# Message passing over 400,000 edges on one core: the last 23 supertiles' messages kept in DRAM, three slot tables in turn, 0/1 rows made by ScalarE

## The chip, the core and the metric

The kernel runs on one core of a Trainium2 chip. The metric is the device time of one execution in microseconds (us); three runs of the kernel before lie within 7 us of each other. The core's engines work side by side, each through its own instructions in order: PE (TensorE, matrix products, with PEld its weight loads), DVE (VectorE), ACT (ScalarE), POOL (GpSimd) and SP (SyncE, which here only issues transfers). Transfers run on 16 DMA engines and are issued by SP, by ACT and, where rows go to computed addresses, by POOL.

## What is computed

Nodes are 12,500 rows of 128 numbers, edges 400,000, sorted by `dst`:

```python
h   = relu(layernorm(x)) @ W_in2f.T
Wij = (smu(f_ij @ W_f1.T + b_f1) @ W_f2.T + b_f2) * rcut_ij[:, None]
agg = segment_sum(h[dst] * Wij, src, 12500)      # gathered by dst, summed by src
out = x + smu(agg @ W_o1.T + b_o1) @ W_o2.T + b_o2
# smu(z) = ((1+a) z + (1-a) z erf(mu (1-a) z)) / 2, a = 0.01, mu = 2.5
```

The edges are sorted by the index of the gather, so that one needs only a narrow window of `h`; the sum goes by the random index `src`.

## The kernel before

**Tiles.** 128 edges are a tile (3125 of them), four tiles a group (`GRP`, 782 groups), eight tiles a supertile (`SUP`, 391). Supertiles are cut into nine epochs by `PARTS` (59 supertiles each at first, 16 in the last). 128 nodes are a bin (98 bins).

**One edge group.** `load` (L432) brings the edge attributes, the row of relative targets (`rbc`) and a window of `h` by the SP queue. `pick` (L465) compares the row with the partition number (`prow`; `pcol` for the first six supertiles) into a 0/1 matrix `oh`, once for a supertile, on DVE (L472). `gather` (L585) multiplies the window by it on PE, `take` (L600) copies the result to SBUF on ACT. `hide`, `bend`, `smooth`, `weigh` (L556 to L617) make the filter: PE, ACT (Gelu), DVE, PE. `mix` (L621) multiplies both on DVE. `turn` (L630) multiplies each tile by `w_o1` on PE, which also brings edges onto partitions. `send` (L639) scales by the edge weight on ACT into an `ms` buffer (six of them, L642), puts the node's number inside its bin beside it as a 129th column, and has POOL scatter the 128 rows of each tile to their slots by an indirect DMA (L649).

**Slots.** Each epoch has its own DRAM table `buf` (L103) with `CAP[k]` rows for each bin. `bins`, `count`, `read`, `number` (L482 to L552) compute each edge's slot: running counts on DVE, a triangular product on PE, a maximum on DVE. `so` holds the running counts and chains from group to group. The rows that may stay empty are cleared before the epoch by SP from a tile of zeros (`clear`, L168).

**Adding up.** During epoch k the table of epoch k-1 is read back by SP (`fetch`, L673, four chunks ahead), DVE makes a 0/1 selection `se` by comparing the 129th column with `irow_ps` (`choose`, L684) and PE multiplies rows and selection into a bin's sum (`add`, L695: one product for each 128 slots, `Q[k]` of them for a bin), which DVE adds to `agg`. `parts` (L725) spreads these products over the groups of the epoch.

**Order.** The order on PE, DVE, ACT and SP is the program's (L282). The main loop (L901) runs once for each group g: `turn(g)` and `send(g)`, then `number`, `weigh`, `gather`, `take`, some `parts`, `mix` for g+1, `hide`, `bend`, `count`, `smooth` for g+2, `pick` for a supertile ahead, `bins(g+3)`, `read(g+2)`, more `parts`. In epoch 0 a list of `steps` (layernorm and `h` of all nodes, the index rows) is interleaved.

**The end.** After the loop the last epoch's table is added up (L960 to L1044), and each unit of four bins goes through Gelu on ACT, an addition on POOL (L1000), `w_o2` on PE, an addition on DVE and its store. The old rows `x` of 12 units are read ahead during the last epoch (`ahead`, L928), the others by ACT's queue at the end; POOL adds the output bias to them (L250).

Of the kernel before, what the change touches and what calls it, by code (L numbers as in the profile page):

```python
# [9 lines left out]
F32 = mybir.dt.float32  # L10
# [9 lines left out]
P = 128  # L20
# [11 lines left out]
PARTS = (59, 59, 59, 59, 48, 37, 27, 27, 16)  # L32
# [8 lines left out]
def gnn_kernel(  # L41
# [46 lines left out]
    for a, n in eps_of:  # L88
        mean = n * SUP * P * P / N
        dev = SIGMA * math.sqrt(mean)  # L90
        CAP.append(math.ceil((mean + dev) / P) * P)
        ZMIN.append(max(0, math.floor((mean - dev) / ZP) * ZP))
# [10 lines left out]
    bufs = [dram.tile([NB * CAP[k], ROW], F32, name=f"buf{k}") for k in range(EPOCHS)]  # L103
# [17 lines left out]
    nc.vector.tensor_add(prow, prow, late)  # L121
    irow = const.tile([P, P], F32, name="irow")
# [19 lines left out]
    b1w = const.tile([P, P], F32, name="b1w")  # L142
# [14 lines left out]
    b2row = const.tile([1, P], F32, name="b2row")  # L157
    b1 = const.tile([P, 1], F32, name="b1")
    bz = const.tile([P, 1], F32, name="bz")
    w_o1 = const.tile([P, P], F32, name="w_o1")  # L160
# [4 lines left out]
    zero = const.tile([ZP, CB * max(c - z for c, z in zip(CAP, ZMIN)) * ROW // ZP], F32, name="zero")  # L165
# [109 lines left out]
    with tc.tile_pool(name="ld", bufs=4) as ld, \  # L275
# [8 lines left out]
        irow_ps = ps1.tile([P, GRP * P], F32, name="irow_ps")[:, 0:P]  # L284
# [138 lines left out]
        def last_loads():  # L423
            nc.sync.dma_start(b2row, b_f2)
            nc.sync.dma_start(bo2, b_o2.to_broadcast([P, P]))

        groups = [(t0 + a, g) for t0, nt in sups for a, g in chunks(nt, GRP)]
        epoch = [k for k, (a, n) in enumerate(eps_of) for _ in range(n)]
# [3 lines left out]
        def load(s):  # L432
            if s >= NS:
                return
            t0, nt = sups[s]
            e0, n = t0 * P, nt * P
            fb = fbufs[s % NF]
# [28 lines left out]
        def pick(s):  # L466

            if s >= NS:
                return
            n = sups[s][1] * P  # L470
            oh = edge.tile([P, SUP * P], BF, name="oh", bufs=3)
            nc.vector.tensor_scalar(oh[:, :n], loaded[s][1][:, :n], pcol if s < FEW // SUP else prow, None, op0=ALU.is_equal)  # L472
            onehot[s] = oh

        last = {}
        begins = {}

# [4 lines left out]
        def bins(g):  # L482


            if g >= NG:
                return
            t, n = groups[g]
            so = cnt.tile([P, GRP, NB], F16, name="so")
            if g in first:
                k = first[g]  # L490
                m = FEW if g == 0 else tiles_of(k)
                begins[k] = (t, cnt.tile([P, max(n for _, n in eps_of) * SUP], F32, name="hic", bufs=2))
                nc.vector.tensor_scalar(begins[k][1][:, :m], hi_f[:, t:t + m], float(CAP[k]), -BIG, op0=ALU.mult, op1=ALU.add)
                last[0] = none
            before = last[0]
# [3 lines left out]
            last[0] = so[:, n - 1]  # L499
            bins_of[g] = (before, so)  # L500
# [43 lines left out]
        def number(g):  # L544
            if g >= NG:
                return
            (t, n), k = groups[g], epoch[g // PER]
            t0, hic = begins[k]
            ix = cnt.tile([P, GRP], I32, name="ix", bufs=8)
# [80 lines left out]
        def turn(g):  # L630

            n = groups[g][1]
            pt = ps1.tile([P, GRP, P], F32, name="pt")
            mt = mixed.pop(g)
            for j in range(n):
                nc.tensor.matmul(pt[:, j, :], mt[:, j * P:(j + 1) * P], w_o1, start=True, stop=True)  # L636
            mixed[g] = pt

        def send(g):  # L639
# [3 lines left out]
            nc.scalar.activation(ms[:, :n, P], lo_b[:, t:t + n], AF.Copy)  # L643
            pt = mixed.pop(g)
            for j in range(n):
                nc.scalar.activation(ms[:, j, 0:P], pt[:, j], AF.Copy, scale=w_sb[:, t + j:t + j + 1])  # L646
            k, ix = epoch[g // PER], taken.pop(g)
# [36 lines left out]
        def choose(k, c):  # L684
# [6 lines left out]
            nc.vector.tensor_tensor(se[:, :m], irow_ps.unsqueeze(1).to_broadcast([P, m, P]),  # L691
# [3 lines left out]
        def add(k, b, q):  # L695
# [15 lines left out]
            if g == GRP - 1 or b == NB - 1:  # L711
                dst = agg[:, (b - g) * P:(b + 1) * P]
                src = pgs[0][:, :g + 1].rearrange("p b n -> p (b n)")
                if k == 0:
                    nc.vector.tensor_copy(dst, src)
                else:
                    nc.vector.tensor_add(dst, dst, src)  # L717

# [15 lines left out]
        def homes():  # L734
            spent = eps_of[-1][0] * SUP // (GRP * P) * (GRP * P)
            for t in (w_sb, hi_f):
                for o in range(0, spent, GRP * P):
                    yield t[:, o:o + GRP * P]
            for o in range(0, spent // 2 // (GRP * P) * (GRP * P), GRP * P):
                yield lo_w.bitcast(F32)[:, o:o + GRP * P]  # L740

        held = {unit: home.rearrange("p (b d) -> p b d", b=GRP)
                for unit, home in zip([u for u in units if u[1] == GRP][::2], homes())}
        ahead = list(held)
# [85 lines left out]
        def output_bias():  # L830

            nc.vector.tensor_scalar(w_o2, w_o2, GC, None, op0=ALU.mult)
            nc.vector.tensor_scalar(bz, b1, ZS, None, op0=ALU.mult)
            nc.vector.tensor_scalar(b1w, onesb, b1, LIN, op0=ALU.mult, op1=ALU.mult)
            pb1 = bank("pb1")[:, 0, :]
            nc.tensor.matmul(pb1, b1w, w_o2, start=True, stop=True)
# [64 lines left out]
        for g in range(NG):  # L901
            s = g // PER
            k = epoch[s]
            g0, ng = eps_of[k][0] * PER, min(eps_of[k][1] * PER, NG - eps_of[k][0] * PER)
            i = g - g0
            if g == (FEW // SUP - 3) * PER:
                assert not opening
            if g % PER == 0:
                load(s + 3)
# [7 lines left out]
            elif k + 1 < EPOCHS:  # L917
# [5 lines left out]
            if k and i == 0:  # L923
                work = [(b, q) for b in range(NB) for q in range(Q[k - 1])]
                done = 0
# [4 lines left out]
            if k and k == EPOCHS - 1 and i >= WAIT and ahead:  # L930
                unit = ahead.pop(0)
                old_rows(unit, held[unit], nc.sync)
            lo = hi = 0
# [4 lines left out]
            if g:  # L938
# [3 lines left out]
            number(g + 1)  # L942
            weigh(g + 1)
            gather(g + 1)
            take(g + 1)
            parts(k - 1, lo + (hi - lo) // 2)
            mix(g + 1)
            step()
            hide(g + 2)
            bend(g + 2)  # L950
            count(g + 2)
            smooth(g + 2)
            if g % PER == 0:
# [5 lines left out]
            assert k == 0 or taken_steps == COUNT  # L959
        k = EPOCHS - 1  # L960
# [5 lines left out]
        small = [u for u in units if u[0] >= NB // GRP * GRP]  # L966
        row_of, ready, opened, smoothed, summed = [], [], [], [], []
        wanted = small + [u for u in units if u not in small]

        def ask():  # L970
            if wanted:
                unit = wanted.pop(0)
                name = ("hg", "mt")[len(wanted) % 2]
                if unit in held:
                    xr = held[unit]
                else:
                    xr = edge.tile([P, GRP * P], F32, name=name).rearrange("p (b d) -> p b d", b=GRP)
                    old_rows(unit, xr, nc.scalar)
                with_bias(unit, xr, nc.gpsimd)
                row_of.append((unit, xr))  # L980
# [28 lines left out]
        def store():  # L1009
            unit, py = summed.pop(0)  # L1010
            was, xr = row_of.pop(0)
            assert was == unit
            stored(unit, py, xr, msg.tile([P, GRP, ROW], F32, name="ms")[:, :, 0:P], nc.sync)
            ask()

        while ahead:
            unit = ahead.pop(0)
            old_rows(unit, held[unit], nc.sync)
        for _ in range(4):
            ask()  # L1020
# [40 lines left out]
    with tc.If(flag > 0):  # L1061
        with tc.tile_pool(name="gl", bufs=1) as gl, tc.tile_pool(name="gps", bufs=1, space=PSUM) as gps:
# [3 lines left out]
            for b, n in chunks(N + P, P):  # L1066
                nc.sync.dma_start(tab[b:b + n, :], zt[:n])
            drop = gl.tile([P, 1], F32, name="drop")
# [125 lines left out]
```

## Time and profile before

| | |
|---|---|
| median of 3 runs | 4111.01 us (4106.05 to 4113.0) |
| the profiled execution | 4114.52 us |
| its span, first to last instruction | 4112.7 us |
| granted TensorE clock, mean | 0.976 |
| HBM read, written | 442.34 MB, 373.37 MB |

The span is what the views of the profile divide up; the 1.8 us between it and the execution's time lie outside the first and last instruction. A row of a view by lines names source line, engine, operation, tiles out and in, shapes and count, then busy time in us and the mean ns of one, then the idle time ahead of it with what ended it. A row of a view by windows has busy time and number of instructions for each engine in that stretch, the clock, the DMA engines' mean share and the GB/s moved. In a timeline the first two columns are start and duration in us.

### The profile page before, as it was taken

The numbers are of one execution on the slowest core, as the hardware profiler recorded it, in microseconds if no ns is written. First come the engines' busy times: TensorE is split into PE (matmuls) and PEld (weight loads), VectorE is DVE, ScalarE is ACT, GpSimd is POOL, SyncE is SP. The second block draws the span as 40 slices with busy tenths as digits, with TensorE's granted clock in tenths as the row PEclk, the third lists the DMA queues.
The fourth block names the chain that finished last, engine by engine and source line by source line (L and its number), as shares of the span: only waits on it lengthen the run. The fifth ranks groups of instructions, "written<-read, shape, count | busy, mean of one in ns | idle before, by whom it ended". The sixth has DMA issues, their size and how long they took to land.

```text
span 4112.7 us, 74065 instructions
## 1 busy us (share of the span) xinstructions
PE 3675.1 (89%) x21113; PEld 2552.3 (62%) x21117; DVE 3450.5 (84%) x7657; ACT 1944.9 (47%) x5690; POOL 3096.4 (75%) x3199
## 2 busy tenths in 40 slices
PE   7878887999888998979999979999899989999898
PEld 4445545666655666646666656666677767666678
DVE  8988776888878888868888868888799979888897
ACT  4457754444444444435444434444444434444442
POOL 6777777777777777777777777777777777777775
PEclk9999998999999999989999989999999999999999
DMA  6866656766647666646766647777688789887668
GB/s 187 231 187 182 191 166 183 213 202 195 188 141 219 198 201 197 199 146 196 212 199 187 199 148 207 210 204 211 176 228 223 195 230 242 221 228 221 176 195 248
DMA packets 564245, 820.83 MB, mean 200 GB/s; under 512 B 178033, under 2 KB 378488, under 8 KB 563698
## 3 DMA queue, kind: packets, MB, share of 16 engines
q1 hardware_dynamic: 456096, 604.98, 53.5%
q0 software_dynamic: 100320, 207.40, 15.7%
q10 hardware_dynamic: 7410, 3.65, 0.3%
q8 instruction: 167, 2.74, 0.3%
q14 instruction: 252, 2.06, 0.2%
HBM read 442.34 MB, written 373.37 MB: 198 GB/s over the span
## 4 chain that ended last, share of the span: by engine, by line
PE 39%; DVE 29%; DMA 18%; ACT 6%; issue 5%; POOL 2%; DVEq 0%; ACTq 0%; POOLq 0%; SPq 0%
DMA buf<-ms,ix 17%; PE pt L636 11%; PE pg L704 9%; PE pw L616 8%; DVE se L691 8%; PE pu L563 7%; DVE mt L626 5%; DVE so L497 5%; DVE sm L579 3%; DVE sl L541 3%; ACT ge L571 2%; ACT ms L646 2%; PE ph L597 2%; POOL buf L649 2%; DVE agg L717 1%
## 5 line engine op out<-in xcount | busy, mean ns | idle before, releaser
L649 POOL DMA_INDIRECT buf<-ms,ix x3125 | 3025.4, 968 | 972.7 <-issue 395.9
L646 ACT ACTIVATE ms<-pt,w_sb 128x128 f32<-128x128 f32 x3125 | 888.8, 368 | 1125.5 <-PE pt L636 1118.0
L636 PE MATMUL pt<-w_o,mt 128*128 128x128 f32 x6250 | 881.3, 284 | 390.9 <-DVE mt L626 388.4
L704 PEld LDWEIGHTS pg<-se,rw 128*128 128x128 f32 x8036 | 1052.4, 192 | 249.7 <-issue 210.8
L704 PE MATMUL pg<-se,rw 128*128 128x128 f32 x8036 | 1148.8, 280 | 4.5 <-DVE se L691 3.7
L636 PEld LDWEIGHTS pt<-w_o,mt 128*128 128x128 f32 x6250 | 765.5, 193 | 478.7 <-DVE mt L626 474.5
L497 DVE SCALAR_TENSOR_TENSOR so<-irow_ps,hi_f,so 128x98 f16<-128x98 f32 x3116 | 989.0, 317 | 82.7
L616 PE MATMUL pw<-sm,w_f 128*128 128x512 f32 x1564 | 826.7, 611 | 10.4 <-DVE sm L579 8.5
L563 PE MATMUL pu<-f,w_f 128*128 128x512 f32 x1564 | 811.4, 601 | 0.0
L626 DVE SCALAR_TENSOR_TENSOR mt<-pw,b,hg 128x512 f32<-128x512 f32 x782 | 583.6, 746 | 207.3 <-ACT hg L605 203.8
L571 ACT ACTIVATE ge<-pu 128x512 f32<-128x512 f32 x782 | 468.6, 599 | 532.7 <-PE pu L563 526.5
L579 DVE SCALAR_TENSOR_TENSOR sm<-pu,ge 128x512 f32<-128x512 f32 x782 | 535.3, 684 | 187.8 <-ACT ge L571 182.0
L691 DVE TENSOR_TENSOR se<-irow_ps,rw 128x1536 f32<-128x1536 f32 (+1 forms) x345 | 587.9, 1704 | 114.3 <-DMA rw<-buf 110.2
L605 ACT ACTIVATE hg<-ph 128x512 f32<-128x512 f32 x782 | 468.6, 599 | 62.1 <-PE ph L597 44.9
L541 DVE TENSOR_REDUCE sl<-pc 128x4 f32<-128x392 f32 x782 | 434.7, 556 | 0.0
L643 ACT ACTIVATE ms<-lo_b 128x4 f32<-128x4 bf16 x782 | 159.9, 204 | 358.7 <-DMA buf<-ms,ix 358.2
L597 PE MATMUL ph<-oh,hw 126*128 126x512 bf16 x770 | 298.3, 387 | 0.0
L563 PEld LDWEIGHTS pu<-f,w_f 128*128 128x128 f32 x1564 | 253.5, 196 | 53.4 <-issue 43.8
L511 PE MATMUL pc<-so,tri 128*128 128x392 f16 x782 | 257.9, 330 | 1.0 <-DVE sl L541 0.8
L616 PEld LDWEIGHTS pw<-sm,w_f 128*128 128x128 f32 x1564 | 241.1, 195 | 24.7 <-DVE sm L579 21.4
L513 PEld LDWEIGHTS <-rest_h 128*128 128x128 f16 x781 | 76.5, 98 | 265.9 <-issue 265.9
L513 PE MATMUL pc<-so,rest_h 128*128 128x294 f16 x781 | 225.1, 288 | 0.0
(161 smaller groups left out, 1391.0 us busy)
## 6 DMA issues: line engine op xcount, KB each, us to landing
rw<-buf SPq DMA_DIRECT2D x292, 774.0 KB
rbc<-rel_dram SPq DMA_DIRECT2D x389, 256.0 KB
buf<-zero SPq DMA_DIRECT2D x243, 387.0 KB
buf<-ms,ix POOLq DMA_INDIRECT x3125
buf<-zero SPq DMA_DIRECT2D x193, 258.0 KB
rw<-buf SPq DMA_DIRECT2D x49, 645.0 KB
f<-in_f_t SPq DMA_DIRECT2D x390, 80.0 KB
hw<-h_dram SPq DMA_DIRECT2D x770, 31.5 KB
```

The costliest lines, as they stand in the source:

```text
L497: nc.vector.scalar_tensor_tensor(so[:, j], irow_ps[:, :NB], hi_f[:, t + j:t + j + 1], so[:, j - 1] if j else before, op0=ALU.is_equal, op1 ...
L541: nc.vector.tensor_reduce(sl[:, :n], pc[:, :n], op=ALU.max, axis=AX.X)
L563: nc.tensor.matmul(pu[:, :n], w_f1, loaded[g // PER][0][:, o:o + n], start=True, stop=True)
L571: nc.scalar.activation(ge[:, :n], units_of[g][:, :n], AF.Gelu, scale=ZS)
L579: nc.vector.scalar_tensor_tensor(sm[:, :n], units_of.pop(g)[:, :n], LIN, hidden[g][:, :n], op0=ALU.mult, op1=ALU.add)
L616: nc.tensor.matmul(pw[:, :n], w_f2, hidden.pop(g)[:, :n], start=True, stop=True)
L626: nc.vector.scalar_tensor_tensor(mt[:, :n], pws.pop(g)[:, :n], b2, rows_of.pop(g)[:, :n], op0=ALU.add, op1=ALU.mult)
L636: nc.tensor.matmul(pt[:, j, :], mt[:, j * P:(j + 1) * P], w_o1, start=True, stop=True)
L646: nc.scalar.activation(ms[:, j, 0:P], pt[:, j], AF.Copy, scale=w_sb[:, t + j:t + j + 1])
L649: i = nc.gpsimd.indirect_dma_start(out=bufs[k][:, :], out_offset=bass.IndirectOffsetOnAxis(ap=ix[:, j:j + 1], axis=0), in_=ms[:, j, :], in ...
L691: nc.vector.tensor_tensor(se[:, :m], irow_ps.unsqueeze(1).to_broadcast([P, m, P]), rows_in[c][:, :m, P:P + 1].to_broadcast([P, m, P]), op= ...
L704: nc.tensor.matmul(pgs[0][:, g, :], rows_in[c][:, o, 0:P], sel[c][:, o, :], start=(q == 0), stop=(q == Q[k] - 1))
```

## The change

There are ten epochs; the last two (`SENT_LAST`), 16 and 7 supertiles, 181 tiles, are "kept". Their groups are computed in the main loop, one supertile after every ninth of supertiles 59 to 265 (`flow`), and their message rows are written by ACT's DMA queue to `kept_rows` in DRAM; their slot numbers stay in `ix_kept`. After the main loop the rows are read back by SP (`refill`), POOL scatters them, and during that the tables of epochs 7 and 8 are added up. The tables are three stores used in turn; a mark added to the 129th column (`mark`, `marks`) tells the rows of an epoch from older ones, so only the first three epochs clear. The 0/1 rows `oh` are made by ACT as relu(1 - |row - prow|), two passes for a group, from the seventh supertile on. Messages that aren't kept are only transposed by PE (`turn`), and `w_o1` is applied to `agg` at the end of epoch 7 (`fold`). All old rows and the bias for them come ahead of the end, the bias on DVE.

```diff
-PARTS = (59, 59, 59, 59, 48, 37, 27, 27, 16)
+PARTS = (59, 59, 59, 59, 48, 37, 27, 20, 16, 7)
+SENT_LAST = 2
+BUFS = 3
...
-    bufs = [dram.tile([NB * CAP[k], ROW], F32, name=f"buf{k}") for k in range(EPOCHS)]
+    stores = [dram.tile([NB * CAP[k], ROW], F32, name=f"buf{k}") for k in range(min(BUFS, EPOCHS))]
+    bufs = [stores[k % BUFS][0:NB * CAP[k], :] for k in range(EPOCHS)]
...
+        flow, rest_of = [], list(range(EARLY, NS))
+        start, gap = eps_of[1][0], (eps_of[5][0] - eps_of[1][0]) // (NS - EARLY)
+        for s in range(EARLY):
+            flow.append(s)
+            if s >= start and (s - start) % gap == gap - 1 and rest_of:
+                flow.append(rest_of.pop(0))
+        flow += rest_of
...
-            rb = ld.tile([P, SUP * P], BF, name="rbc")
+            rb = ld.tile([P, SUP * P], BF, name="rbc", bufs=3)
...
+        def pick_part(g):
...
+            s, i = divmod(g, PER)
+            if s < FEW // SUP:
+                if i == 0:
+                    pick(s)
+                return
+            if i == 0:
+                onehot[s] = edge.tile([P, SUP * P], BF, name="oh", bufs=3)
+            o, n = i * GRP * P, groups[g][1] * P
+            oh = onehot[s][:, o:o + n]
+            nc.scalar.activation(oh, loaded[s][1][:, o:o + n], AF.Abs, bias=nrow)
+            nc.scalar.activation(oh, oh, AF.Relu, scale=-1.0, bias=onesb[:, 0:1])
...
             for j in range(n):
-                nc.tensor.matmul(pt[:, j, :], mt[:, j * P:(j + 1) * P], w_o1, start=True, stop=True)
+                if s_of(g) < EARLY:
+                    nc.tensor.transpose(pt[:, j, :], mt[:, j * P:(j + 1) * P], ident)
+                else:
+                    nc.tensor.matmul(pt[:, j, :], mt[:, j * P:(j + 1) * P], w_o1, start=True, stop=True)
...
+            if s_of(g) >= EARLY:
+                nc.scalar.dma_start(kept_rows[:, t - kept_tile:t - kept_tile + n, :], ms[:, :n, :])
+                return
+            scatter(g, ms)
...
+        def fold():
+
+            dst = plain.pop(0)
+            w = dst.shape[1]
+            po = ps1.tile([P, GRP * P], F32, name=("pu", "ph")[len(folded) % 2])
+            nc.tensor.matmul(po[:, :w], w_o1, dst, start=True, stop=True)
+            nc.scalar.activation(dst, po[:, :w], AF.Copy)
+            folded.append(w)
...
-            elif k + 1 < EPOCHS:
+            elif k + 1 < BUFS:
...
+            if s < EARLY:
+                k = chores(g)
+            else:
+                lo = hi = done
...
-            if g % PER == 0:
-                pick((g + 4) // PER)
-            bins(g + 3)
-            read(g + 2)
+            pick_part(at(p + 4))
+            bins(at(p + 3))
+            read(at(p + 2))
...
+        def refill(g):
+            if g < NG:
+                t, n = groups[g]
+                back[g] = msg.tile([P, GRP, ROW], F32, name="ms")
+                nc.sync.dma_start(back[g][:, :n, :], kept_rows[:, t - kept_tile:t - kept_tile + n, :])
+
+        g1 = EARLY * PER
+        for g in range(g1, g1 + 4):
+            refill(g)
+        for g in range(g1, NG):
+            refill(g + 4)
+            k = chores(g)
+            scatter(g, back.pop(g))
+            parts(k - 1, hi)
+            if g - g1 >= 2:
+                old(g - g1 - 2)
+            biased(g - g1 - 10)
```

`chores(g)` holds what stood at the head of the loop's body: clearing, the beginning of an epoch and the share of `parts` due in group g. `scatter` is the second half of what `send` did.

More of the change, by code (lines that the diff above doesn't have):

```diff
@@ L91, in gnn_kernel @@
         CAP.append(math.ceil((mean + dev) / P) * P)
-        ZMIN.append(max(0, math.floor((mean - dev) / ZP) * ZP))
+        ZMIN.append(max(0, math.floor((mean - dev) / ZP) * ZP) if len(ZMIN) < BUFS else 0)
+    assert all(c <= CAP[k % BUFS] for k, c in enumerate(CAP)) and (EPOCHS - 1) // BUFS < GRP
     Q = [c // P for c in CAP]
@@ L121, in gnn_kernel @@
     nc.vector.tensor_add(prow, prow, late)
+    nrow = const.tile([P, 1], F32, name="nrow")
+    nc.vector.tensor_scalar(nrow, prow, -1.0, None, op0=ALU.mult)
     irow = const.tile([P, P], F32, name="irow")
@@ L487, in bins @@
             t, n = groups[g]
-            so = cnt.tile([P, GRP, NB], F16, name="so")
+            kept = s_of(g) >= EARLY
+            so = cnt.tile([P, GRP, NB], F16, name="so_kept" if kept else "so", bufs=2 if kept else 3)
             if g in first:
@@ L937, in gnn_kernel @@
                 hi = upto * (i + 1 - WAIT) // (ng - WAIT)
-            if g:
+            return k
+        k = 0
+        for p in range(len(seq)):
+            g = seq[p]
+            s = g // PER
+            if p == (FEW // SUP - 3) * PER:
+                assert not opening
+            if p % PER == 0:
+                load(sup_at(p // PER + 3))
+            if s < EARLY:
+                k = chores(g)
+            else:
+                lo = hi = done
+            if p:
                 turn(g)
@@ L963, in gnn_kernel @@
         choose(k, order_of[k][0])
[L966 to L980, printed above, removed]
+        ready, opened, smoothed, summed = [], [], [], []
         turns = [0, 0]
@@ L1010, in store @@
             unit, py = summed.pop(0)
-            was, xr = row_of.pop(0)
+            was, xr = rows_got.pop(0)
             assert was == unit
             stored(unit, py, xr, msg.tile([P, GRP, ROW], F32, name="ms")[:, :, 0:P], nc.sync)
[L1014 to L1020, printed above, removed]
         for c in order_of[k]:
```

139 lines of the change are left out of this document (91 added, 48 removed).

## Prediction

> **What bounds the kernel now.** I read the page first, then the scatter alone, then single iterations. The page's shares mislead:
>
> ```profile
> PE 3675.1 (89%) x21113; PEld 2552.3 (62%) x21117; DVE 3450.5 (84%) x7657; ACT 1944.9 (47%) x5690; POOL 3096.4 (75%) x3199
> L649 POOL DMA_INDIRECT buf<-ms,ix x3125 | 3025.4, 968 | 972.7 <-issue 395.9
> ```
>
> PE looks the fullest and POOL idles 972.7 us. The timeline of POOL alone, and the scatter's own view with windows, say otherwise:
>
> ```profile
> 1999.34 0.96 POOL L649 DMA_INDIRECT buf<-ms,ix  x1 [0.30 <-issue]
> 2000.61 0.96 POOL L649 DMA_INDIRECT buf<-ms,ix  x1 [0.30 <-ACT ms L643]
> 2001.87 0.96 POOL L649 DMA_INDIRECT buf<-ms,ix  x1 [0.31 <-DMA buf<-ms,ix]
> L649 POOL DMA_INDIRECT buf<-ms,ix x3125: 956/962/1460, 19.9 to 4022.2; - x196
> 20.00:560.00 540.00, 404.92 (x414) 0.97 0.70 198
> 560.00:3400.00 2840.00, 2159.04 (x2235) 0.98 0.68 195
> 3400.00:3870.00 470.00, 355.60 (x368) 0.99 0.80 218
> 3870.00:4024.00 154.00, 105.78 (x110) 1.00 0.71 201
> ```
>
> A scatter starts every 1.265 us: 0.96 busy and 0.30 of idle time that recurs whatever is named as its releaser, so it belongs to the instruction. 3124 such periods are 3952 us; the first scatter starts at 19.9, the last at 4022.2, so only 50 us in 4002 are anything else. Stage by stage (length less count x 1.265): 16 us to 560, 13 to 3400, 4.5 to 3870, 14 in the last epoch (to 4023). The engines' loads differ between epochs, the scatter does not:
>
> ```profile
> 2000.00:2500.00 500.00, 441.62 (x2525) 306.57 (x2525) 404.84 (x890) 226.63 (x676) 380.32 (x394) 0.97 0.63 187
> 3000.00:3500.00 500.00, 477.41 (x2915) 347.36 (x2914) 441.77 (x932) 230.00 (x679) 378.06 (x393) 0.98 0.85 223
> ACT ms L643 <- DMA buf<-ms,ix: 358.2, 163, 6.2
> ```
>
> PE goes from 441.62 to 477.41 us in 500, POOL does 394 and 393 scatters. The third row, of the waits, is the back pressure: ACT waits 358 us for one of the six `ms` buffers to be scattered. So POOL is the bound until 4022, and then a tail of 90 us follows, without scatters. Whatever the change saves on PE and DVE in the main loop is worth nothing by itself; it counts where POOL stands still, where a scatter is stretched, and in the tail.
>
> **The change, part by part.**
>
> *POOL's work*: 3125 scatters as before, 2944 in the main loop, 181 behind it; 0 us. The clears that go (some 89 MB, by SP) lay beside POOL: 0.
>
> *The comparison leaves DVE.* What stretches a scatter shows in single places:
>
> ```profile
> 1302.27 1.22 POOL L649 DMA_INDIRECT buf<-ms,ix  x1 [0.30 <-issue]
> 1302.18 0.48 DVE L472 TENSOR_SCALAR oh<-rbc,prow 128x1024 bf16<-128x1024 bf16 x1
> ```
>
> The scatter that begins 0.09 us into a comparison takes 1.22 us, not 0.96. All stretching together is at most 3025.4 - 3125 x 0.962 = 19 us; by the windows some 6.5 of it lies before 560, where other DVE work stretches too. From 560 on it is 2159.04 + 355.60 - 2603 x 0.962 = 11 us. I take a gain of 13 (8 to 19).
>
> The Trainium skill, page "SBUF — State Buffer", section "Who interferes with whom", says that a VectorE instruction in a 2-port mode and GpSimd exclude each other, the later one blocking fully. Held for a whole comparison (0.48 us) on each of 385, that would be a gain of some 185 us; the measured stretch of 19 us in all decides against that size, while the trace agrees with the sign.
>
> *ACT gets two passes for each group.* No row shows this operation. The nearest:
>
> ```profile
> L353 ACT ACTIVATE hs<-pg 128x512 bf16<-128x512 f32 x6 | 3.6, 595 | 0.0
> L994 ACT ACTIVATE ge<-agg,bz 128x512 f32<-128x512 f32 x24 | 17.0, 721 | 52.2 <-DVE ms L268 22.1 <-POOL hg L250 16.8 <-DVE agg L717 7.2
> L226 ACT ACTIVATE hs<-rw 128x512 bf16<-128x512 f32 x23 | 14.9, 647 | 1.8 <-DVE rw L223 1.8
> ```
>
> So 1.19 to 1.44 us for two; I take 1.3, by L226 (source and target in SBUF). They stand behind `bend` on ACT, and the next `send` is queued behind them.
>
> *PE transposes.* The turn's row has two instructions for a tile, a transpose one:
>
> ```profile
> 2005.47 1.06 PE L636 MATMUL pt<-w_o,mt 128*128 128x128 f32 x8
> 304.66 0.60 PE L211 MATMUL pg<-ident,rw 128*128 128x128 f32 x4
> 2006.36 1.02 PE L616 MATMUL pw<-sm,w_f 128*128 128x512 f32 x2
> 2012.12 0.59 PE L616 MATMUL pw<-sm,w_f 128*128 128x512 f32 x1
> ```
>
> Eight passes are issued in 0.89 us (2005.47 to 2006.36), 0.111 each; four transposes, 0.60 in all, need half. PE saves 0.45 us for each early group: hidden behind POOL.
>
> *Is the loop fast enough for POOL?* Eighteen early groups give POOL 18 x 4 x 1.265 = 91.1 us of work, but beside them two kept groups are computed: twenty iterations in 91.1 us, 4.55 each. Per iteration (98.5 in the window 2000 to 2500):
>
> ```profile
> L704 PE MATMUL pg<-se,rw 128*128 128x128 f32 x978 | 145.3, 281 | 0.0
> L472 DVE TENSOR_SCALAR oh<-rbc,prow 128x1024 bf16<-128x1024 bf16 x48 | 23.9, 498 | 0.0
> L691 DVE TENSOR_TENSOR se<-irow_ps,rw 128x1536 f32<-128x1536 f32 x41 | 71.8, 1752 | 19.1 <-DMA rw<-buf 18.9 <-PE pg L704 0.2
> L717 DVE TENSOR_TENSOR agg<-agg,pg 128x512 f32<-128x512 f32 (+1 forms) x21 | 14.0, 667 | 0.7 <-PE pg L704 0.7
> ```
>
> PE 441.62/98.5 = 4.48, less 0.45: 4.03; DVE 4.11 less 23.9/98.5: 3.87; ACT 2.30 + 1.3 = 3.60. Kept iterations have no `parts` but the old turn: PE 4.48 less 978 x 0.111/98.5 = 1.1, that is 3.4, DVE 4.11 - 0.24 - 0.87 = 3.0. Over twenty, PE asks 3.97 (87% of 4.55), DVE 3.78 (83%), ACT 3.60 (79%). Before, at POOL's 5.08, the shares were 88%, 81% and 45%, with 0.46 us of back pressure for each iteration (358/782). So POOL just stays fed; I take 0, and up to +90 if the chain through the fuller ACT lengthens iterations (first rival).
>
> *Epoch 0.* There ACT also makes `h`:
>
> ```profile
> 300.00:560.00 260.00, 221.54 (x1130) 137.84 (x1129) 209.07 (x506) 192.41 (x538) 198.17 (x204) 0.99 0.64 188
> ```
>
> 51 groups x 1.3 us on 192.4 busy make 259 of 260 us: ACT becomes the bound. At nine tenths of its time (PE reaches 0.88 and 0.95 in the windows above) the stretch takes some 288 us, 28 more; up to 30 us of it (24 scatters waiting in six `ms` buffers) is absorbed. Between 0 and +30 I take +10.
>
> *The last epochs.* The 14 us lost after 3870 came from 258 `add` products in 28 groups, 9.2 each, when PE could not keep up. The densest stage of the main loop now is 294 in 36, 8.2, with 0.45 us less of other PE work; I take 5 of 14, and beside it the 4.5 us before 3870 as now: gain 9 (0 to 14).
>
> *The refill.* Behind the loop 181 x 1.265 = 229 us of scatters go on, each fed from DRAM. SP's queue holds the refills and the table reads in one order, and a table read waits for PE; POOL has four groups (20 us) ahead. By the size of a chunk (below, 1536 rows) epochs 7 and 8 read 19.4 and 12.9 MB, refills 12.0, old rows 6.4, scatters 12.0: 62.7 MB in 229 us, 274 GB/s.
>
> ```profile
> 4031.00:4108.00 77.00, 68.60 (x585) 67.10 (x584) 59.03 (x68) 17.68 (x26) 44.61 (x37) 0.98 0.90 273
> rw<-buf SPq DMA_DIRECT2D x292, 774.0 KB
> ```
>
> The tail of before moved 273 GB/s at 0.90 of the DMA engines' time: full would be 303. At 223 GB/s and 0.85 (the window from 3000), full is 262, and the stage takes 239. So 0 to +35; I take +5.
>
> *The tail.* It runs from the last scatter to the end:
>
> ```profile
> 4022.18 0.96 POOL L649 DMA_INDIRECT buf<-ms,ix  x1 [0.30 <-issue]
> 4031.55 1.76 DVE L691 TENSOR_TENSOR se<-irow_ps,rw 128x1536 f32<-128x1536 f32 x1 [1.46 <-DMA rw<-buf]
> ```
>
> 9.4 us until the last table's rows are there, then 81 to the span's end for 25 units, of which I put 75, 3.0 each, to the units and 6 to draining. A unit was 16 passes of `add` and 8 of `w_o2` on PE, 24 x 0.111 = 2.7 us, and 0.53 MB of table, 0.26 out and 0.26 of old rows. With one product for a bin it is 16 passes, 1.8 us; on DVE 0.69 + 0.69 + a third of a `se` 0.58 = 1.96; 0.53 MB at 303 GB/s 1.75. I take 2.0: 9.4 + 50 + 6 = 65, a gain of 25 (15 to 32).
>
> **Sum** against the profiled execution, 4114.5: -13 + 10 - 9 + 5 - 25 = -32, and of the 16 us lost before 560 and the 4.5 later nothing else moves: 4082. The median of the runs shown is 3.5 lower than that execution: 4079.
>
> **The rivals.**
>
> 1. *ACT takes POOL's place between supertiles 68 and 265* (slower). A comparison of 1.3 us now stands between `bend` and the next `send`; where DVE's `se` (1.75 us) makes `mix` late, ACT has little left to catch up: the gap ahead of `send` is about as long as the two passes.
>
> ```profile
> 2006.56 0.63 ACT L646 ACTIVATE ms<-pt,w_sb 128x128 f32<-128x128 f32 x2 [1.27 <-PE pt L636]
> ```
>
> Price: 23 stretches x (18 e + 2 x 3.8 - 91.1) for an early iteration of e. It starts to cost at 4.64 us and makes the kernel slower than before at 4.73 (40/23/18 more). At 4.85 it is 23 x 3.8 = 87: 4166. For it: the iteration with a `se` from 2006.36 to 2012.12, above, took 5.76 us. Against it: PE's 0.45 and DVE's 0.24 us less.
>
> 2. *The refill stage is bound by transfers.* At the profile's mean of 200 GB/s, 62.7 MB take 313 us, not 229: 4158. For it: rows get shorter, three and two slots a partition. Against it: 273 GB/s in the tail now.
>
> 3. *The tail and the stretching don't follow*: the tail stays bound by latencies, and other DVE work stretches scatters as much. Without 25 of the 38 gained: 4104.
>
> 4. *Abs, Relu and Gelu in turn reload ACT's tables.*
>
> ```profile
> L413 ACT ACT_TABLE_LOAD x1 | 1.3, 1283 | 2.6 <-issue 2.6
> ```
>
> Two for each group would be 776 x 2 x 1.28 = 1990 us on ACT, over its slack by far: about 5500. Only four loads stand in this trace, though Copy and Gelu alternate; that is the case against. The Trainium skill, "ScalarE: Activation LUTs", section "Table sets: the hidden batching unit", has relu, abs, copy and identity in every set, and by that rule no load is added; no run so far shows Abs.
>
> **How the numbers follow.** Forecast 0.62 (4050 to 4103), rival 1 0.18, rival 2 0.08, rival 3 0.11, rival 4 0.01. The low end takes the gains' upper bounds with 0 for epoch 0 and the refill: 4114.5 - 19 - 14 - 32 - 3.5 = 4046. Up to 4130 it holds rival 3 and the weaker part of 1 and 2; about 0.17 is left above. A difference of 0.2% (8 us) is what can be told from none. Faster: the forecast's 0.62, half of rival 3 and the mild cases of 1 and 2, 0.74; same 0.06; slower 0.20.
>
> **What would show it.** Right: scatters at 1.265 us from 70 us to the last, none stretched by a comparison; the last scatter near 4011; PE's and DVE's busy shares down with no effect on that; no table loads; a tail of 65 us. Wrong: periods over 1.3 us between about 650 and 2700, with POOL's idle time ended by ACT's `ms` (rival 1) or by refills behind the loop (rival 2). A POOL period other than 1.265 in undisturbed stretches would take away the whole sum.

## The result, and the profile after

The changed kernel takes 4066.85 us (median of 5 runs, 4061.25 to 4071.34), the kernel before beside it 4108.48 (5 runs, 4104.56 to 4113.0): ratio 0.9898, 95% interval 0.9884 to 0.9913. The forecast was 4079 (4046 to 4130). The profiled execution took 4064.05 us, its span is 4062.2.

The page of the changed kernel, busy time of each engine, then the scatter's own view (count, min/median/max ns, first and last start) and its windows; the scatter now stands at L714, twice, the second time for the kept tiles:

```profile
PE 3500.9 (86%) x18417; PEld 2253.0 (55%) x18420; DVE 3331.9 (82%) x7344; ACT 2959.9 (73%) x7255; POOL 3039.7 (75%) x3173
L714 POOL DMA_INDIRECT buf<-ms,ix x2944: 952/958/1417, 19.4 to 3762.8; - x197
L714 POOL DMA_INDIRECT buf<-ms,ix_kept x181: 954/958/1462, 3764.1 to 3993.8; - x181
20.00:560.00 540.00, 403.18 (x418) 0.95 0.74 198
560.00:3400.00 2840.00, 2143.61 (x2239) 0.98 0.62 179
3400.00:3764.00 364.00, 275.97 (x289) 0.97 0.64 183
3764.00:3996.00 232.00, 175.73 (x181) 0.84 0.89 266
```

ACT went from 1945 to 2960 us busy, and the kernel got faster: POOL still sets the time. Its last scatter starts at 3993.8 and not 4022.2, 28 us earlier; from there to the end it is 68 us and not 90.5, 22 less. The period between undisturbed starts is 1.2625 us, some 3 ns shorter than before (958 ns busy in the median and not 962). That is 8 of the 28 us, and I don't put it down to the change: one and the same kernel, run three times below, had 962 (e1) and 958 (e9, e11). It fits that the profiled execution of before lay 6 us above its median and this one 3 below. By medians the change is worth 41.6 us.

The two passes that ACT now makes, its four table loads, and PE's iteration (timeline):

```profile
L512 ACT ACTIVATE oh<-oh,onesb 128x512 bf16<-128x512 bf16 x769 | 555.1, 722 | 25.2
L511 ACT ACTIVATE oh<-rbc,nrow 128x512 bf16<-128x512 bf16 x769 | 550.8, 716 | 10.5 <-DMA rbc<-rel_dram 10.5
L423 ACT ACT_TABLE_LOAD x1 | 1.3, 1283 | 2.6 <-issue 2.6
L864 ACT ACT_TABLE_LOAD x1 | 1.3, 1283 | 0.0
L206 ACT ACT_TABLE_LOAD x1 | 1.3, 1283 | 0.0
L621 ACT ACT_TABLE_LOAD x1 | 1.3, 1283 | 0.0
1095.25 0.60 PE L687 MATMUL pt<-ident,mt 128*128 128x128 f32 x4
1095.75 1.12 PE L666 MATMUL pw<-sm,w_f 128*128 128x512 f32 x2
1096.71 0.38 PE L647 MATMUL ph<-oh,hw 126*128 126x512 bf16 x1
```

A pass takes 0.72 us, at the upper end of what was assumed. There are four table loads, as before: rival 4 is out, and by that the trace agrees with the Trainium skill, "ScalarE: Activation LUTs", "Table sets: the hidden batching unit". Four transposes are issued in 0.50 us (1095.25 to 1095.75), but the product after them takes 0.96 to the next one and not 0.86 (2006.36 to 2007.22 before): the shortest iteration with ten passes of `add` went from 4.35 to 4.06 us, 0.29 less and not 0.45.

POOL's longest stop in the stretch with kept supertiles (timeline of POOL), then what the windows of all engines show for epoch 0:

```profile
2449.81 0.96 POOL L714 DMA_INDIRECT buf<-ms,ix  x1 [0.30 <-issue]
2455.03 0.96 POOL L714 DMA_INDIRECT buf<-ms,ix  x1 [4.26 <-ACT ms L703]
300.00:560.00 260.00, 203.07 (x910) 111.60 (x910) 195.19 (x469) 252.25 (x637) 197.79 (x205) 0.98 0.66 186
```

There are five such stops, 2 to 4 us each, near 1106, 1267, 2451, 2546 and 2640. In the last four POOL had run out of messages: each begins 1 to 3 us behind the last `turn` of a kept supertile, when every message that ACT had finished was scattered. At 1106 twelve finished messages were waiting; the kernel before has two such stops, of about 2 us at 167 and 3405, and their cause is open. In epoch 0 ACT is busy 252 of 260 us, and POOL did 205 scatters, one more than before.

In the tail, DVE's first `se` of the last table and one unit of four bins on PE (timelines):

```profile
3993.76 0.96 POOL L714 DMA_INDIRECT buf<-ms,ix_kept  x1 [0.31 <-issue]
4002.70 1.76 DVE L757 TENSOR_TENSOR se<-irow_ps,rw 128x1536 f32<-128x1536 f32 x1 [1.35 <-DMA rw<-buf]
4023.34 1.06 PE L273 MATMUL pw<-w_o,sm 128*128 128x128 f32 x8
4024.23 1.06 PE L770 MATMUL pg<-se,rw 128*128 128x128 f32 x8
4025.12 1.06 PE L273 MATMUL pt<-w_o,sm 128*128 128x128 f32 x8
```

8.9 us to the first rows, then a unit every 1.78 us (4023.34 to 4025.12), and 2.4 where PE waits 0.45 us for POOL's addition `sm`; 25 units end at 4054.

The views of the kernel before hold one thing more that the change touched. POOL's timeline in the old last epoch, and its instructions from 3870 to 4024:

```profile
3874.65 0.96 POOL L649 DMA_INDIRECT buf<-ms,ix  x1 [0.30 <-issue]
3875.63 2.50 POOL L250 TENSOR_TENSOR w_sb<-w_sb,bo 128x512 f32<-128x512 f32 x2
3878.30 0.98 POOL L649 DMA_INDIRECT buf<-ms,ix  x1 [0.17 <-issue]
L250 POOL TENSOR_TENSOR w_sb<-w_sb,bo 128x512 f32<-128x512 f32 x5 | 6.4, 1283 | 0.1
L250 POOL TENSOR_TENSOR hi_f<-hi_f,bo 128x512 f32<-128x512 f32 x5 | 6.3, 1276 | 0.1
L250 POOL TENSOR_TENSOR lo_b<-lo_b,bo 128x512 f32<-128x512 f32 x2 | 2.6, 1283 | 0.0
```

Between two scatters POOL itself adds the output bias to old rows that were read ahead. These twelve additions fill all nine stops of that epoch, 14 us, and four finished messages were waiting at each. The change gives the additions to DVE.

### The profile page after: what moved, and what is told of

It reads as the page before. It is cut to its first block, busy times and chain, and to the rows that moved or that the text cites. A ratio compares the mean times of both kernels' runs of the same rounds, so it can differ in the third digit from the quotient of the medians.

```text
span 4062.2 us, 69833 instructions
## 1 busy us (share of the span) xinstructions
PE 3500.9 (86%) x18417; PEld 2253.0 (55%) x18420; DVE 3331.9 (82%) x7344; ACT 2959.9 (73%) x7255; POOL 3039.7 (75%) x3173
## 4 chain that ended last, share of the span: by engine, by line
PE 42%; DVE 26%; DMA 13%; ACT 9%; issue 5%; POOL 4%; ACTq 0%; DVEq 0%; SPq 0%; POOLq 0%
PE pw L666 13%; DMA buf<-ms,ix 10%; PE pg L770 10%; DVE se L757 9%; PE pu L613 7%; PE pt L687 7%; DVE mt L676 5%; POOL buf L714 4%; DVE sl L588 3%; ACT ms L703 3%; ACT ge L621 2%; DVE sm L629 2%; PE ph L647 2%; DVE so L544 2%; DMA rw<-buf 2%
## 5 line engine op out<-in xcount | busy, mean ns | idle before, releaser
L714 POOL DMA_INDIRECT buf<-ms,ix x2944 | 2823.4, 959 | 930.8 <-issue 260.4
L770 PEld LDWEIGHTS pg<-se,rw 128*128 128x128 f32 x8232 | 1085.0, 195 | 339.5 <-issue 282.3
L770 PE MATMUL pg<-se,rw 128*128 128x128 f32 x8232 | 1179.6, 283 | 93.5 <-DVE se L757 81.6
L544 DVE SCALAR_TENSOR_TENSOR so<-irow_ps,hi_f,so 128x98 f16<-128x98 f32 x2936 | 929.7, 317 | 78.1
L666 PE MATMUL pw<-sm,w_f 128*128 128x512 f32 x1564 | 885.4, 649 | 47.5 <-DVE sm L629 46.7
L687 PE MATMUL pt<-ident,mt 128*128 128x128 f32 x2944 | 469.3, 282 | 356.5 <-DVE mt L676 354.7
L512 ACT ACTIVATE oh<-oh,onesb 128x512 bf16<-128x512 bf16 x770 | 555.5, 721 | 25.2
L687 PEld LDWEIGHTS pt<-ident,mt 128*128 128x128 f32 x2944 | 327.5, 142 | 441.0 <-DVE mt L676 437.6
L511 ACT ACTIVATE oh<-rbc,nrow 128x512 bf16<-128x512 bf16 x770 | 551.2, 716 | 10.5 <-DMA rbc<-rel_dram 10.5
L558 PE MATMUL pc<-so,tri 128*128 128x392 f16 x736 | 243.6, 331 | 0.6 <-DVE so L544 0.6
```

The source lines that it names most:

```text
L512: nc.scalar.activation(oh, oh, AF.Relu, scale=-1.0, bias=onesb[:, 0:1])
L666: nc.tensor.matmul(pw[:, :n], w_f2, hidden.pop(g)[:, :n], start=True, stop=True)
L687: nc.tensor.transpose(pt[:, j, :], mt[:, j * P:(j + 1) * P], ident)
L714: i = nc.gpsimd.indirect_dma_start(out=bufs[k][:, :], out_offset=bass.IndirectOffsetOnAxis(ap=ix[:, j:j + 1], axis=0), in_=ms[:, j, :], in ...
L770: nc.tensor.matmul(pgs[0][:, g, :], rows_in[c][:, o, 0:P], sel[c][:, o, :], start=(q == 0), stop=(q == Q[k] - 1))
```

## The experiments

Theory: POOL's scatters set the time up to the last one, so what counts is that a scatter isn't stretched, that POOL never runs dry, and what follows the last scatter. Rivals: PE and DVE set it; ACT does; the full lock between DVE's comparison and POOL.

The chips differed. e5 to e8 and e11 ran where the kernel before took 4103 us; e1 to e4, e9, e10 and e12 ran on chips where it took 5015 to 5098. What those show is told at each, and at the end. The changed kernel as it is was not run on those chips. No run undoes the move of the bias additions alone.

**e1, e9, e11: the comparison back on VectorE** (three runs of one kernel).

```diff
-            nc.vector.tensor_scalar(oh[:, :n], loaded[s][1][:, :n], pcol, None, op0=ALU.is_equal)
+            nc.vector.tensor_scalar(oh[:, :n], loaded[s][1][:, :n], pcol if s < FEW // SUP else prow, None, op0=ALU.is_equal)
...
-            nc.scalar.activation(oh, loaded[s][1][:, o:o + n], AF.Abs, bias=nrow)
-            nc.scalar.activation(oh, oh, AF.Relu, scale=-1.0, bias=onesb[:, 0:1])
+                pick(s)
```

> The changed kernel with the comparison back on VectorE, one instruction for a supertile. Theory (POOL's scatters are the bound, a comparison on DVE stretches those that begin during it): scatters of 1.0 to 1.25 us come back, some 11 to 14 us in all, and the loop is otherwise as fast; 4067 + 13 = 4080, with up to 20 more if DVE's 0.24 us for an iteration was what kept the stretch with kept supertiles fed. Rival (the full lock: each comparison holds POOL for its whole 0.48 us): 4067 + 185 = 4250. Rival (ACT's two passes cost as much as they save): 4067 or less.

> The same kernel as e1 (the changed one with the comparison back on VectorE), since e1 to e4 ran on a chip on which the kernel before takes 5082 us and POOL waits for ACT at every turn, so that their ratios don't bear on the question. Theory (POOL-bound, a comparison stretches the scatters that begin during it): from 560 us on some 120 to 145 scatters over 975 ns again, 15 us in all, and scatters of 960 ns and not 957.6, 8 us: 4067 + 15 to 25 = 4085 (4075 to 4100). Rival (full lock): 4250. Rival (no gain from the move): 4067 or less.

> Once more the changed kernel with the comparison on VectorE (e1, e9 ran on chips on which POOL isn't the bound). Where POOL is the bound: some 120 to 145 stretched scatters after 560 us, 15 us in all, scatters of 960 ns, 8 us, and perhaps longer stops in the stretch with kept supertiles: 4085 (4075 to 4100). Rival (full lock): 4250. Rival (no gain): 4067 or less. On a chip where the kernel before takes 5080 or more: again 2.7 to 2.9% slower than it, because 181 scatters follow a loop that POOL didn't bound.

Where POOL is the bound (e11): 4080.17 us, 0.9943 of the kernel before (0.9929 to 0.9956), against 0.9898 for the changed kernel: 13 us by the medians, 18 by the ratios. Three stretched scatters of e11 between 2000 and 2100, from the timeline of POOL, and its two windows; the second covers the stretch with kept supertiles:

```profile
2002.97 1.13 POOL L706 DMA_INDIRECT buf<-ms,ix  x1 [0.30 <-issue]
...
2022.08 1.03 POOL L706 DMA_INDIRECT buf<-ms,ix  x1 [0.30 <-issue]
...
2086.57 1.17 POOL L706 DMA_INDIRECT buf<-ms,ix  x1 [0.30 <-issue]
20.00:560.00 540.00, 404.56 (x416) 0.94 0.68 200
560.00:2700.00 2140.00, 1613.83 (x1677) 0.99 0.59 177
```

Taking every scatter over 975 ns, from 560 us on: 121 in the kernel before, 12 in the changed one, 91 in e11, 79 of which overlap a comparison. Over the whole execution such scatters exceed the median by 23.3, 6.6 and 19.4 us. So the move is worth the 13 us between the last two, and the full lock (4250) falls, as does "no gain". In the stretch with kept supertiles e11 did 1677 scatters where the changed kernel did 1685 (below), 10 us: 8 of stretching and 2 of longer stops.

On the other chips (e1, e9) the same kernel takes 5230.11 and 5250.89 us, 1.0277 (1.0236 to 1.0317) and 1.0287 (1.025 to 1.0323) of the kernel before. What POOL waits for in e1, and its scatters:

```profile
POOL buf L706 <- ACT ms L695: 1209.9, 494, 13.5
L706 POOL DMA_INDIRECT buf<-ms,ix x2944: 955/962/1404, 19.9 to 4856.6; - x197
L706 POOL DMA_INDIRECT buf<-ms,ix_kept x181: 956/962/1427, 4857.9 to 5159.2; - x181
```

POOL waits 1210 us for messages, so it isn't the bound there; 181 scatters then follow the loop for 301 us. That keeping messages back is what costs time there is argued from this; no run separates it from the other parts.

**e2, e10: the 0/1 rows by ScalarE in the kernel before, nothing else.** `pick_part` comes with it, as in the change.

```diff
...
-            if g % PER == 0:
-                pick((g + 4) // PER)
+            pick_part(g + 4)
```

> The kernel before with only the 0/1 rows moved to ScalarE in two passes. Theory: no scatter after the first 70 us is stretched by a comparison, 13 us less; the main loop stays at POOL's pace since ACT has 2.3 + 1.4 of 5.06 us to do; 4108 - 13 = 4095. Rival (ACT becomes the bound in epoch 0, where it also makes h): up to 28 us more, 4123. Rival (the fuller chain through ACT slows the PE-limited last epoch): some 10 us more than 4095.

> The same kernel as e2 (the one before with only the 0/1 rows moved to ScalarE), on another chip. Theory: 15 us of stretched scatters go and up to 10 us by scatters of 957 ns; the loop stays at POOL's pace: 4108 - 20 = 4088 (4080 to 4098). PE's turn is the old one there, but without kept supertiles an iteration has 5.05 us. Rival (the chain through the fuller ACT lengthens iterations beyond 5.05 us even so): 4108 or more.

Both ran on the slower chips: 5216.05 us, 1.0269 (1.0233 to 1.0304), and 5228.42, 1.0256 (1.0223 to 1.0289). Stretching after 560 us goes there too (7 scatters in e2), but POOL waits 1263 us for ACT, and the 1.1 ms more of work on ACT lengthens the loop. What the part is worth alone where POOL is the bound wasn't measured; e11 gives it within the change.

**e3, e12: only the small last epoch, in the kernel before.**

```diff
-PARTS = (59, 59, 59, 59, 48, 37, 27, 27, 16)
+PARTS = (59, 59, 59, 59, 48, 37, 27, 20, 16, 7)
```

> The kernel before with the ten epochs of the change (the last of 7 supertiles), nothing else. Theory: the tail shrinks by some 22 us as in the changed kernel, but the products of the last tables must be done beside full iterations: in the epoch of 16 supertiles 10.5 a group, 5.6 us against 5.06, 15 us lost; in that of 7, 16 a group, 6.8 us, 18 us lost; the 14 us lost in the old last epoch go: 4108 - 22 + 15 + 18 - 14 = 4105. Rival (the small last epoch by itself is the gain, and keeping messages adds nothing): 4086.

> The same kernel as e3 (the one before with the ten epochs of the change), for a chip where POOL is the bound. Theory as for e3: a tail shorter by some 22 us, but 33 us of stops of POOL in the last two epochs, where PE has 10.5 and 16 products of add for each group beside full iterations, instead of 14: 4103 - 22 + 33 - 14 = 4100 (4090 to 4112). Rival (the small last epoch by itself is the gain): 4081. On a chip where the kernel before takes 5080 or more: no difference, as in e3.

Both on the slower chips: 1.001 (0.9982 to 1.0039) and 1.003 (1.0008 to 1.0052), no gain. In e12's trace the tail is 84 us (last scatter 4979.0, end 5063.2) against 68 in the changed kernel. POOL's additions in that tail, and what PE waits for there (a row has the total in us, the number and the longest):

```profile
L1000 POOL TENSOR_TENSOR sm<-agg,ge 128x512 f32<-128x512 f32 (+2 forms) x26 | 30.8, 1203 | 16.0 <-ACT ge L994 16.0
L250 POOL TENSOR_TENSOR hg<-hg,bo 128x512 f32<-128x512 f32 (+1 forms) x13 | 15.7, 1210 | 4.4 <-DMA hg<-in_x 4.4
PE pu L264 <- POOL sm L1000: 6.9, 6, 2.2
PE pw L264 <- POOL sm L1000: 4.6, 5, 1.2
```

POOL makes 20 us of bias additions (L250) beside `sm`, and PE waits 13 us for `sm`. In the changed kernel, where the bias is done ahead, PE waits 2.6 us for it. That speaks against the small epoch as the gain by itself; on a chip where POOL is the bound it wasn't measured. Both expectations also count on the 14 us of the old last epoch going; as seen above these are POOL's own additions, which this edit leaves on POOL.

**e4: kept supertiles not spread but one after another at the end of the loop.**

```diff
-            if s >= start and (s - start) % gap == gap - 1 and rest_of:
-                flow.append(rest_of.pop(0))
```

> The changed kernel with the 23 kept supertiles computed one after another at the end of the main loop and not spread between the others. Theory: POOL has nothing to scatter during 46 iterations of about 3.9 us, less the 20 to 25 us of scatters that wait in buffers: 4067 + 46 x 3.9 - 23 - 12 (the stops between 1100 and 2650 go) = 4210. Rival (the gain doesn't hang on where the kept groups are computed, since PE and DVE are the bound and their work is the same): 4067 within 10.

Again a slower chip: 5256.14 us, 1.032 (1.0274 to 1.0366), little above e1's and e9's kernels there. The timeline of POOL shows the price that was expected, and the window of all engines whose time it is:

```profile
4710.35 0.96 POOL L712 DMA_INDIRECT buf<-ms,ix  x1 [0.30 <-issue]
4888.70 0.95 POOL L712 DMA_INDIRECT buf<-ms,ix_kept  x1 [177.39 <-issue]
4720.00:4880.00 160.00, 130.06 (x605) 73.86 (x603) 120.03 (x308) 141.11 (x342) 0.00 (x0) 1.00 0.33 108
```

POOL stands still for 177 us. On that chip the loop isn't POOL's anyway, so spreading gains little; that it would cost 140 us on the other chips is argued from this stop, not measured.

**e5: `w_o1` in the turn again, for every tile.** It takes the `fold` away too.

```diff
-                if s_of(g) < EARLY:
-                    nc.tensor.transpose(pt[:, j, :], mt[:, j * P:(j + 1) * P], ident)
-                else:
-                    nc.tensor.matmul(pt[:, j, :], mt[:, j * P:(j + 1) * P], w_o1, start=True, stop=True)
+                nc.tensor.matmul(pt[:, j, :], mt[:, j * P:(j + 1) * P], w_o1, start=True, stop=True)
...
-                if k == EPOCHS - SENT_LAST - 1:
-                    plain.append(dst)
-                    if len(plain) > 1:
-                        fold()
```

> The changed kernel with w_o1 applied to every tile in the turn again, no fold at the end of epoch 7. PE does 0.3 us more for each early iteration (4.35 against 4.06 with ten passes of add). Theory (POOL bound, but with only 40 us of back pressure left in all, so the transposition is what keeps POOL fed in the stretch with kept supertiles): 18 x 0.3 = 5 us for each of 23 stretches less the slack there, 4067 + 50 (20 to 90), all of it as POOL's idle time between 650 and 2750. Rival (POOL bound with room to spare): 4067 within 5.

4104.65 us, 1.0005 (0.9996 to 1.0014): the gain is gone, 38 us by medians, 44 by the ratios. The window from 560 to 2700 of the scatter in the changed kernel, then the same window of e5, e6 and e7:

```profile
560.00:2700.00 2140.00, 1612.64 (x1685) 0.98 0.62 179
```

```profile
560.00:2700.00 2140.00, 1584.86 (x1655) 0.99 0.58 176
```

```profile
20.00:560.00 540.00, 389.07 (x403) 0.91 0.65 188
560.00:2700.00 2140.00, 1605.64 (x1677) 0.99 0.59 179
```

```profile
560.00:2700.00 2140.00, 1619.46 (x1691) 0.98 0.59 177
```

2140 us hold 1695 scatters of 1.2625 us. The changed kernel misses 10 of them, e5 misses 40: 30 x 1.2625 = 38 us, the whole difference by medians. In e5's trace they are 19 stops of POOL, most of them 93 us apart, as the kept supertiles are. So a saving of 0.3 us for each iteration on an engine that isn't the bound over the whole loop decides the result, because among the kept supertiles it decides how often POOL runs dry.

**e6: a third pass on ACT over the 0/1 rows.**

```diff
             nc.scalar.activation(oh, oh, AF.Relu, scale=-1.0, bias=onesb[:, 0:1])
+            nc.scalar.activation(oh, oh, AF.Relu)
```

> The changed kernel with a third pass of 0.72 us on ScalarE over the 0/1 rows of each group (a Relu that changes nothing). It measures the room on ACT. Theory: ACT asks 3.9 + 0.7 = 4.6 of 4.55 us in the stretch with kept supertiles and becomes the bound there and in epoch 0: 4067 + 60 to 150. Rival (PE and DVE are what paces the loop, ACT has room): under 4080.

4094.21 us, 0.9977 (0.9967 to 0.9987): 27 us more than the changed kernel by medians, 32 by the ratios, between the two expectations; neither came true. By the windows above 15 scatters (19 us) are lost before 560, where ACT also makes `h`, and 8 (10 us) from there to 2700. So ACT is at its limit in epoch 0 and has more room than PE among the kept supertiles: 0.72 us more for each group on ACT costs 10 us there, 0.3 more on PE 38.

**e7: a kept supertile after every eleventh, not every ninth.**

```diff
-        start, gap = eps_of[1][0], (eps_of[5][0] - eps_of[1][0]) // (NS - EARLY)
+        start, gap = eps_of[1][0], (eps_of[6][0] - eps_of[1][0]) // (NS - EARLY)
```

> The changed kernel with a kept supertile after every eleventh and not every ninth: 24 iterations in 22 x 5.05 = 111 us, 4.63 for one and not 4.55. Theory: of the stops of POOL between 1100 and 2650 (17 us) most go, those in epoch 4 above all (11 us there): 4067 - 8 = 4059 (4054 to 4064). Rival (epochs 5 and 6, with denser products, now lose as much): 4067.

4055.96 us (4052.66 to 4057.66), 0.9882 (0.9866 to 0.9897): 11 us below the changed kernel by medians, but only 7 by the ratios, and the intervals of the two ratios overlap, so that it is the faster of the two isn't shown by the times. By the window 1691 scatters and not 1685 are done to 2700, 7.6 us, and POOL's stops there shrink from 14 to 5 us, as expected.

**e8: every second scatter of epochs 3 to 7 left out.**

```diff
-            for j in range(n):
+            for j in range(0, n, 2 if 3 <= k < EPOCHS - SENT_LAST else 1):
```

> The changed kernel with every second scatter left out in epochs 3 to 7 (half of their messages never reach a table, so the sums lack them). It shows the pace of the loop without POOL. Theory: 191 supertiles and the kept ones between go from 5.05 us for an early group to the pace of PE, DVE and ACT, 4.4 to 4.7 for all iterations: some 100 to 200 us less, 3870 to 3970, and no more, since the second bound is near. Rival (another resource is the bound): 4067 within 10. Rival (much room behind POOL): under 3800.

A single run: 3974.54 us, just outside the range; 764 scatters less, 965 us of POOL's time, bring 92. All engines from 1820 to 3500 in e8 (PE, PEld, DVE, ACT, POOL):

```profile
1820.00:3500.00 1680.00, 1574.20 (x8579) 1032.39 (x8578) 1491.55 (x3223) 1350.19 (x3278) 665.29 (x696) 1.00 0.52 159
```

PE is busy 94% of the time, DVE 89%, POOL 40% (696 periods of 1.2625 us are 52%). Both extreme rivals fall: POOL was the bound, and the next bound lies close behind it.

## Why the prediction was right

**POOL is the bound until the last scatter: right.** PE's and DVE's busy time fell by 174 and 119 us; the last scatter came 28 us earlier. e8 shows how close the next bound is. The prediction named a period other than 1.265 us as what would take away its sum. It was 1.2625, which moves the sum by 8 us between the two profiled executions and leaves the rest as it is.

The table splits the 50.5 us between those two executions by the terms of the sum. The time from one scatter's start to the next, less the undisturbed period, is divided into stretching and stops:

| Term | Forecast, us | Profiles, us |
|---|---|---|
| stretched scatters | -13 | -17 |
| stops in epoch 0 | +10 | 0 |
| stops from 560 to 3400, with kept supertiles | 0 | +13 |
| stops in the last epochs | -9 | -17 |
| refill | +5 | 0 |
| tail | -25 | -22 |
| period | 0 | -8 |
| sum | -32 | -51 |

Without the period it is -43; by medians it is -41.6.

**The comparison stretches scatters: right, a little small.** 13 was predicted (8 to 19); the traces give 23.3 - 6.6 = 17, e11 13 to 18. "At most 19" for all stretching was wrong: it took the median for every undisturbed scatter, and many are a little shorter. The trace agrees with the rule of the Trainium skill ("SBUF — State Buffer", "Who interferes with whom") that the later of the two blocks: a scatter that begins during a comparison is longer by what is left of the comparison, less 0.13 us (last section). What was wrong in the 185 us is that each comparison would cost its whole 0.48 us. After 560 us, 88 scatters were stretched by a comparison that began ahead of them, by 0.15 us on average; a scatter that began first was stretched little or not at all.

**Epoch 0: wrong in size.** +10 was taken, 0 measured: the window to 560 holds 418 scatters, four more than before, and the stops are as long. The assumption that failed is that ACT would reach nine tenths; it reached 252 of 260, and what it lacked was covered by messages waiting. e6, with 0.72 us more, lost 19 us at once: right in kind.

**The last epochs: the gain was too small, and the cause was wrong.** The prediction put the 14 us lost after 3870 down to PE, which couldn't keep up with the products of `add`, and took 5 of them as a gain. But those stops are POOL's own twelve bias additions (section on the result), while four finished messages waited each time. The change moves them to DVE, and all 14 go. So this term came out on the right side by luck: a part of the change that the sum had nowhere, the bias on DVE, brought it.

**Kept supertiles in the loop: 0 taken, 13 us of stops measured**, the five stops above: 12 behind kept supertiles and 2 at 1106. The step's arithmetic had PE at 87% of what POOL needs. With 0.29 us saved and not 0.45 it was fuller; a kept iteration took 4.23 us in the median, not the 3.4 of PE's work; and iterations with a `se` (4.7 to 5.4 us) leave the six buffers empty after a kept supertile. That is rival 1 at its mild end, by PE and DVE more than by ACT: with PE's saving undone (e5) the whole gain was gone.

**The refill: right.** POOL kept its period; 266 GB/s at 0.89 of the DMA engines' time sufficed. The 2.4 us above 181 periods are scatters stretched by DVE's addition of the bias, and the table counts them as stretching:

```profile
3837.32 0.68 DVE L259 TENSOR_TENSOR f<-f,bo 128x512 f32<-128x512 f32 x1
3837.50 1.33 POOL L714 DMA_INDIRECT buf<-ms,ix_kept  x1 [0.30 <-issue]
```

**The tail: right in size**, 22 us less and not 25. The prediction had it from fewer products and transfers for each unit. By e12's trace the bias additions that left POOL have a share in it too, which no run separates.

The sum came as near as it did because errors offset each other: the stops with kept supertiles (13) and the tail (3) came out worse than was taken, and epoch 0 (10), the last epochs (8), the refill (5) and the stretching (4) better.

## What to carry to other kernels

An engine that shows 75% busy with the same idle gap ahead of every instruction is full: read start to start, not busy time, and count how many instructions it does in stretches with different loads elsewhere. Once that engine is the bound, look for what lengthens its instructions on other engines, and for work that can go behind or between so that it never runs dry; savings elsewhere count only as room for that. When the engine stands still, see first what it does itself in that time: the stops of the last epoch looked like another engine's fault and were its own additions. And check that the bound is the same on the chip at hand: the kernel of e1, e9 and e11 gained 0.6% where POOL was the bound and lost 2.8% where it wasn't.

## What the runs showed of the hardware

- By the sums that follow, a scatter waits out a DVE instruction that was running when it began. In the kernel before, 141 scatters began 0.05 us or more into a comparison (bf16, both sides in SBUF, 0.48 us). 134 of them are longer than the median by what was left of the comparison less 0.13 us, within 0.02 us and by 0.27 us at most, and no longer than the median where less than 0.13 us was left. In the other seven the comparison took 0.52 to 0.54 us and the scatter lost nothing.
- Additions with both inputs in SBUF (0.68 us) do the same: the twelve kept tiles' scatters that began 0.05 us or more into one fit that sum within 0.01 us, the longest 0.50 us over the median (1.46 us).
- It goes the other way too: DVE comparisons that began 0.45 to 0.6 us into a scatter took 0.66 us in the median of 53, not 0.48. Those that began 0.35 to 0.55 us into one stretched it by up to 0.11 us (21 of 68).
- The bare scatter took 962 ns in one execution and 958 in two others of the same kernel (e1; e9, e11); the cause is open.
- On some chips the kernel before took 5015 to 5098 us and not 4103 to 4111. Scatters are as long there (962 ns in e1, 958 in e3), but ACT and others start late: in e3 ACT's `send` waits until 2011.28 though PE's turn ended at 2008.75. The granted TensorE clock was lower there too (0.917 in e3, 0.976 in the profile before). Why is open.

```profile
2007.69 1.06 PE L636 MATMUL pt<-w_o,mt 128*128 128x128 f32 x8
2011.28 1.14 ACT L646 ACTIVATE ms<-pt,w_sb 128x128 f32<-128x128 f32 x4 [3.77 <-PE pu L563]
```

- After four transposes it takes 0.10 us longer from the start of the next fp32 product to the one after it: 0.96 us in 552 of 631 undisturbed cases of the changed kernel, 0.86 in 674 of 714 of the kernel before.
